# A graph network's edge gathers: counting by pairs of chunks, constants loaded ahead, five groups gathered ahead, and a shorter lag of the weights

## The chip, the cores and the metric

The kernel runs on one core of a Trainium2 chip. The core has five engines, each with its own instruction stream taken in order: TensorE (PE, matrix products, with a weight load that runs beside them, PEld), VectorE (DVE), ScalarE (ACT, functions of one operand), GpSimd (POOL, which also issues the indirect transfers that gather rows) and SyncE (SP, which issues most other transfers). They wait for each other through semaphores. Sixteen DMA engines move data between device memory (DRAM), the on-chip SBUF and, through the engines, PSUM. The metric is the device time of one execution in microseconds (us); lower is better.

## The reference, cut to what matters

A graph of 3,125 nodes and 100,000 edges, sorted by destination, with a low index far likelier as a destination than a high one. First a four-layer attention network with 8 heads of 16, then a second message network on the same edges.

```
h = gelu(x @ Wi.T + bi)
for i in range(4):
    q = (h @ Wq.T + bq)[dst]; k = (h @ Wk.T + bk)[src]; v = (h @ Wv.T + bv)[src]
    alpha = sum(q * k over 16) / 4                     # per edge and head
    ex = exp(alpha - segment_max(alpha, dst)[dst])
    out = segment_sum(ex / segment_sum(ex, dst)[dst] * v, dst)
    x_r = h @ Ws.T + bs
    beta = sigmoid([out, x_r, out - x_r] @ Wbeta.T)
    h = layer_norm(beta * x_r + (1 - beta) * out + h)
    h = gelu(h @ W1.T + b1) @ W2.T + b2 + h
x = layernorm(x + h @ Wo.T + bo)
msg = silu([x[src], x[dst], rbf(edge_weight)] @ mw1 + mb1) @ mw2 + mb2
agg = segment_sum(msg, dst) / max(count, 1)
x = layernorm(x + layer_norm(silu([x, agg] @ uw1 + ub1) @ uw2 + ub2))
```

## The kernel before

Nodes lie in 25 tiles of 128 (NT). Edges are cut into items of 256 (`IS`) that all have their destinations in one tile; an item is two chunks of 128 edges, one edge per partition. The lowest four tiles of destinations (DT), which take in many edges each, are treated densely: for them the kernel counts how often each source meets each destination and adds the logarithm of that count as a mask to a full attention of 512 destinations against all nodes. All other edges go through gathers: 246 items (SPI), 123 groups of four chunks (SPG) in each layer.

The stages follow each other in one program.

*Sorting* (`order_edges`, `sort_edges`) brings edges into items, and makes for each chunk of the dense tiles two numbers per edge (`place`, `last`, L452 on): which source row, and which column of a window of DW = 8 low destinations; the window's start for each chunk comes from a masked minimum (L436 to 439).

*Counting* (`count_edges`, L968): for each of 324 chunks POOL makes a one-hot of the source within its tile (`hot_l`, L987), DVE one of source tile times window column (`hot_w`, 25×8 = 200 wide, L990), PE multiplies them (`c_ps`, L993) and DVE adds the product into `cnt` at the window's place (L996), all written in one order with no step ahead of another but by three buffers. Between chunks, seven times, `enter` (L1416) takes four node tiles through the first linear layer, Gelu and the projections to k, v, q and x_r (`project`, `project_rest`). Then 28 blocks of masks are built: transposes of `cnt` on PE, L1008 and L1014 on DVE, L1012 and L1013 on ACT, and stored.

*Layers* (`layers`, L1436). Ahead of the first layer, and at the end of each node stage, the first AHEAD = 4 groups are gathered: four indirect transfers a group, each bringing 128 rows of k and v into a buffer `kvg` (L680). `attention` then runs `edge_sums` (L700), a pipeline by hand. Turn g of `range(-3, ng + LAG + 2)` issues:

```
at(g + 3, fetch)            # gather of group g+3, its row one-hots (hrows)
at(g - LAG - 2, add)        # sums into acc
others(per_turn * (g + 0.5))
at(g, scores)               # qk, alpha (DVE), ev copy of v out of kvg (ACT, L759)
at(g + 1, select)           # q_ps: q rows by one-hot (PE, L742)
advance()                   # one step of the maxima
others(per_turn * (g + 1))
advance()
at(g - LAG + 1, columns)    # hcols
at(g - LAG, weights)        # ev times ex (DVE, L779)
at(g - LAG - 1, by_node)    # products with hcols (PE, L794)
```

Softmax maxima are made for batches of GB = 8 groups by `Maxima.steps` (L559): a generator of some 13 steps, each on another engine than the one before, of which `advance` runs one. It transposes the scores, copies them on ACT (`at`, L577), scans over them on DVE (`fwd`, L581), goes forth and back once more, and ends in the exponentials `ex` (L628). A group's weights are due LAG = GB+6 = 14 turns after its scores. The dense attention (`dense_steps`, L852) is a list of 258 slots, `beside`, spread evenly over the turns by `others`: scores `d_ps` (PE, L878), mask and maximum (DVE, L888), exponentials (ACT, L901), transposes (`pt_ps`, PE, L910), copies (ACT, L917), products with v (L927). In layer 0 the row and column one-hots are made on DVE and stored; layers 1 to 3 load them on SP's queue.

*Node stage* (`node_stage`, L1290): the gate of attention and x_r (`mixing`, with its exponential `beta`, L1077), layer norm, two linear layers with Gelu (L1337, `u`), the next layer's projections. At its start SP loads `lng`, `lnb`, `w1`, `b1`, `w2`, `b2` and the next layer's weights. At its end the next layer's first four groups are gathered, and `project_rest` follows.

*Second network* (`second_network`, `messages`, L1456 on): 204 groups with 816 gathers (L680, `ag`).

The attention stands in two forms under a branch on what sorting found: the one described is taken when the items fit the tables and windows sized for them; the other, general, treats all edges by gathers.

## Time and profile before

| what | us |
|---|---|
| median of three runs (4751.56 to 4760.54) | 4754.53 |
| profiled execution | 4763.96 |
| its span, first to last instruction | 4762.1 |
| sorting, 0 to 83 | 83 |
| counting with entry, 83 to 346 | 263 |
| masks, 346 to 400 | 54 |
| layer 0, first to last gather | 717 |
| layers 1, 2, 3, first to last gather | 667, 661, 667 |
| between the gathers of two layers | 146, 135, 133 |
| from layer 3's last gather to the first of the second network | 146 |
| second network, first to last gather | 1049 |

The stages are read from what each engine does over time; the same lines of code come back four times, once for each layer, and totals mix them. In a window's row the busy time and instruction count of each engine stand in turn; PEclk is the TensorE clock that was granted as a share of full speed; DMA is the mean busy share of the sixteen engines. In a timeline row the brackets hold the engine's idle time just before, and what ended it. In a list of waits the numbers are total, times and longest. A row of a group of instructions has its shortest, median and longest duration in ns.

### The profile page before, as it was taken

How to read it: one execution, taken by the hardware profiler on the slowest of the kernel's cores; microseconds unless marked ns; L12 is line 12 of the kernel's file. 1: busy time of each engine (PE TensorE's matmuls, PEld its weight loads, DVE VectorE, ACT ScalarE, POOL GpSimd, SP SyncE). 2: the span in 40 equal slices, each digit the busy share in tenths (PEclk: the TensorE clock that was granted, in tenths of full speed). 3: DMA queues.
4: the chain of work that ended last, by engine and by line, in shares of the span. 5: the costliest groups of instructions: out<-in, count | busy, mean ns of one | idle time of the engine just before them, and what ended most of it. 6: DMA issues, size and time to landing. Idle time of an engine off the chain costs nothing. (4 is left out here: it accounts for less than half of the span.)

```text
span 4762.1 us, 85370 instructions
## 1 busy us (share of the span) xinstructions
PE 3845.5 (81%) x25947; PEld 2699.6 (57%) x25947; DVE 3246.7 (68%) x10137; ACT 1996.0 (42%) x3967; POOL 2981.0 (63%) x3136
## 2 busy tenths in 40 slices
PE   3666898987889998879999987999887766667775
PEld 1223665665456666546666654666664665666664
DVE  6775898987557987647787855788785444445644
ACT  0014454553345555435555542565543333233321
POOL 4664776762267777147777605777741777777775
PEclk9555998998879999979999996999898888888987
DMA  2005787885467887457887826888762333334432
GB/s 60 27 32 189 230 247 237 249 243 138 144 189 247 258 250 233 114 174 221 246 256 238 221 82 192 245 259 257 229 179 58 97 90 91 92 92 86 97 89 52
DMA packets 451834, 801.33 MB, mean 168 GB/s; under 512 B 93445, under 2 KB 175878, under 8 KB 451296
## 3 DMA queue, kind: packets, MB, share of 16 engines
q1 hardware_dynamic: 329488, 481.40, 31.7%
q0 software_dynamic: 121056, 313.06, 25.7%
q8 instruction: 229, 3.75, 0.3%
q14 instruction: 277, 2.27, 0.2%
q10 hardware_dynamic: 784, 0.85, 0.1%
HBM read 693.93 MB, written 102.26 MB: 167 GB/s over the span
## 5 line engine op out<-in xcount | busy, mean ns | idle before, releaser
L680 POOL DMA_INDIRECT kvg<-kv_d,src_i x1968 | 1955.9, 994 | 880.3 <-issue 567.8
L680 POOL DMA_INDIRECT ag<-a_d,src_i x816 | 797.0, 977 | 254.0 <-issue 226.4
L917 ACT COPY pt<-pt_ps 128x512 f32<-128x512 f32 (+1 forms) x832 | 470.7, 566 | 684.5 <-PE pt_ps L910 677.3
L910 PE MATMUL pt_ps<-ident,sm 128*128 128x128 f32 x3200 | 572.1, 301 | 138.6 <-ACT pt L917 94.1
L742 PE MATMUL q_ps<-q,hrows 128*128 x3936 | 617.2, 303 | 47.6 <-DMA hrows<-hrows_d 21.1
L888 DVE CUSTOM_DVE_ANT_0 sm<-d_ps,mask 128x512 f32<-128x512 f32 (+1 forms) x896 | 541.5, 623 | 143.8 <-PE d_ps L878 119.0
L910 PEld LDWEIGHTS pt_ps<-ident,sm 128*128 128x128 f32 x3200 | 362.6, 148 | 477.8 <-issue 198.7
L742 PEld LDWEIGHTS q_ps<-q,hrows 128*128 128x128 f32 x3936 | 547.0, 213 | 146.2 <-issue 112.7
L878 PE MATMUL d_ps<-kt,qz 32*128 32x512 f32 (+1 forms) x1792 | 602.3, 650 | 7.4 <-DVE mx L888 7.3
L794 PE MATMUL s_ps<-ev,hcols 128*128 128x136 f32 x3744 | 565.9, 294 | 17.5 <-issue 5.5
L901 ACT ACTIVATE sm<-sm,dtop 128x512 f32<-128x512 f32 (+1 forms) x896 | 547.2, 669 | 26.0 <-DVE dtop L895 25.2
L759 ACT COPY ev<-kvg 128x512 f32<-128x512 f32 x492 | 303.5, 618 | 551.9 <-DMA kvg<-kv_d,src_i 351.8
L794 PEld LDWEIGHTS s_ps<-ev,hcols 128*128 128x128 f32 x3744 | 499.5, 200 | 60.8 <-issue 37.8
L1510 PE MATMUL s_ps<-m,hcols 128*128 128x129 f32 x1632 | 277.2, 322 | 256.3 <-DVE acc L1519 234.6
L1502 DVE TENSOR_TENSOR m<-ag,m_ps 128x512 f32<-128x512 f32 x204 | 139.9, 687 | 407.8 <-DMA ag<-a_d,src_i 369.4
L1510 PEld LDWEIGHTS s_ps<-m,hcols 128*128 128x128 f32 x1632 | 248.0, 230 | 292.2 <-ACT m L1503 156.1
L754 DVE TENSOR_TENSOR qk<-q_ps,kvg 128x512 f32<-128x512 f32 x492 | 335.5, 682 | 94.1 <-PE q_ps L742 71.3
L927 PE MATMUL av<-pt,v 128*17 128x128 f32 x6400 | 373.8, 287 | 1.7 <-ACT pt L917 1.7
L810 DVE TENSOR_TENSOR acc<-acc,s_ps 128x136 f32 x936 | 266.4, 285 | 106.2 <-PE s_ps L794 96.8
L779 DVE TENSOR_TENSOR ev<-ev,ex 128x512 f32<-128x512 f32 x492 | 332.5, 683 | 8.9 <-ACT ex L628 8.8
L755 DVE TENSOR_REDUCE alpha<-qk 128x32 f32<-128x512 f32 x492 | 330.8, 672 | 2.3
L1503 ACT ACTIVATE m<-m 128x512 f32<-128x512 f32 x204 | 125.1, 628 | 430.6 <-DVE m L1502 422.6
(316 smaller groups left out, 5247.6 us busy)
## 6 DMA issues: line engine op xcount, KB each, us to landing
mask<-mask_d SPq DMA_DIRECT2D x384, 256.0 KB
hrows<-hrows_d SPq DMA_DIRECT2D x369, 256.0 KB
hcols<-hcols_d SPq DMA_DIRECT2D x369, 256.0 KB
hrow<-drow_d SPq DMA_DIRECT2D x327, 128.0 KB
kvg<-kv_d,src_i POOLq DMA_INDIRECT x1968
hrows_d<-hrows SPq DMA_DIRECT2D x123, 256.0 KB
hcols_d<-hcols SPq DMA_DIRECT2D x123, 256.0 KB
ag<-a_d,src_i POOLq DMA_INDIRECT x816
```

The costliest lines, as they stand in the source:

```text
L680: nc.gpsimd.indirect_dma_start(out=out[:, x, :], out_offset=None, in_=table[:], in_offset=bass.IndirectOffsetOnAxis(ap=s["src_i"][:, i:i + ...
L742: nc.tensor.matmul(qs[g][:, x, :], hot[:, c * P:(c + 1) * P], a["q"][:, bass.ds(tn["PE"][item_of(g, c)], 1), :], start=True, stop=True)
L754: nc.vector.tensor_mul(qk, qs.pop(g), kvg[:, :, :HID])
L779: nc.vector.tensor_mul(e[:, :, :, :DH], e[:, :, :, :DH], ex.unsqueeze(3).to_broadcast([P, IC, GH, DH]))
L794: nc.tensor.matmul(sums[g][:, c // IC], hot[:, c, :], ev[:, ORDER.index(c)].rearrange("p h d -> p (h d)"), start=(c % IC == 0), stop=(c % ...
L878: nc.tensor.matmul(s_ps[i][:, :n * P], qz[r, h % 2, d * P:(d + 1) * P], kt[r, c * P:(c + n) * P], start=True, stop=True)
L888: nc.vector.tensor_tensor_reduce(out=sm[:, i, :n * P], in0=s_ps[i][:, :n * P], in1=mask[:, :n * P], scale=1.0, scalar=-3.0e38, op0=ALU.add ...
L901: nc.scalar.activation(sm[:, i, :n * P], sm[:, i, :n * P], AF.Exp, scale=1.0 / DH ** 0.5, bias=live[u]["top"][:, i:i + 1])
L910: nc.tensor.transpose(t_ps[:, x, y, :], sm[:, y, t % NS * P:(t % NS + 1) * P], k.ident)
L917: nc.scalar.copy(pt[:, :n], live[u]["t_ps"].pop(i)[:, :n])
L927: nc.tensor.matmul(av[r:r + DX, u % len(PAIRS), :], v[:, t, h, :], pt[:, x, y, :], start=(i == 0), stop=(t + 2 >= NT))
L1510: nc.tensor.matmul(s_ps[:, c // IC, :], h[:, c, :], x[:, c, :], start=(c % IC == 0), stop=(c % IC == IC - 1))
```

## The change

1. Counting goes by items of two chunks, 162 of them. DW grows to 10, and there is one window for an item. Its start is no more a masked minimum: four indirect gathers on POOL fetch each chunk's first edge record, and DVE takes the destination out of it. `hot_l` is made on ACT for both chunks: two squares of the distance from iota, with the number as bias (its sign is turned in `place`), and one Relu of 1 − distance over both. `hot_w` is still made per chunk on DVE, 250 wide. Two products accumulate in PSUM and one addition follows. Sources are made two items ahead, places one ahead, additions one behind. `enter` becomes three steps a block, 21 in all, spread evenly.
2. `lng`, `lnb`, `b2`, `b1` for all layers and `w1` of layer 0 are loaded at the start of the program, on POOL's queue; node stages reload `w1` alone, on SP, ahead of the next layer's first gathers. The two DVE operations that prepare `w_out` and `w_xr` of the next layer move from the node stage's beginning to the end of its loop's `late` blocks (`gate`).
3. The first groups of layer 0 are gathered when counting ends, before the masks are built.
4. AHEAD is 5, and the gathers of group g+4 are issued at the head of turn g.
5. 14 dense slots are issued in the first turn, and the remaining 244 spread as before.
6. LAG is 12; a third `advance` runs in each turn; the ev copy moves out of `scores` into `values`, later in the turn.

```
-DW = 8
+DW = 10
...
-LAG = GB + 6
+LAG = GB + 4
...
+        c0 = C0 // P
+        m = NC - c0
+        at_first = one.tile([P, m], I32, name="at_first")
+        nc.vector.scalar_tensor_tensor(at_first, part_f[:, c0:], -3.0 * P, at_edge[:, c0:],
+                                       op0=ALU.mult, op1=ALU.add)
+        first_e = one.tile([P, m, 3], I32, name="first_e")
+        for c in range(m):
+            nc.gpsimd.indirect_dma_start(
+                out=first_e[:, c], out_offset=None,
+                in_=ed_d.rearrange("r s -> (r s)").unsqueeze(1),
+                in_offset=bass.IndirectOffsetOnAxis(ap=at_first[:, c:c + 1], axis=0))
...
-        nc.vector.tensor_scalar(local, ins, -1000.0, 1000.0, op0=ALU.mult, op1=ALU.add)
-        nc.vector.tensor_add(local, local, sl[:, 1, c0:])
         lo = one.tile([P, m], F32, name="lo")
-        nc.vector.tensor_reduce(lo, local, axis=AX.X, op=ALU.min)
+        nc.vector.tensor_copy(lo, first_e[:, :, 1])
+        nc.vector.tensor_sub(lo, lo, tile_f[:, c0:])
...
-        nc.vector.scalar_tensor_tensor(place[:, 0], place[:, 1], -float(P), sl[:, 0, c0:],
-                                       op0=ALU.mult, op1=ALU.add)
+        nc.vector.scalar_tensor_tensor(place[:, 0], place[:, 1], float(P), sl[:, 0, c0:],
+                                       op0=ALU.mult, op1=ALU.subtract)
...
+    def rows_of(g):
         if g >= AHEAD:
             gather_rows(nc, s, a, g)
+    def fetch(g):
...
-        evs[g] = work.tile([P, GC, HEADS, DX], F32, name="ev", bufs=LAG + 3)
-        nc.scalar.copy(evs[g][:, :, :, :DH],
-                       kvg[:, :, HID:].rearrange("p c (h d) -> p c h d", d=DH))
         if b == GB - 1 or g == ng - 1:
             exs[n] = work.tile([P, IC, IB * HEADS], F32, name="ex")
             todo.append((n, maxima.steps(n, exs.pop((n, "alpha")), exs[n])))
+    def values(g):
+        evs[g] = work.tile([P, GC, HEADS, DX], F32, name="ev", bufs=LAG + 3)
+        nc.scalar.copy(evs[g][:, :, :, :DH],
+                       a["kvg"][g % AHEAD][:, :, HID:].rearrange("p c (h d) -> p c h d", d=DH))
...
+    at_once = min(14, len(beside))
+    per_turn = (len(beside) - at_once) / (ng + 4)
...
     for g in turns:
+        at(g + AHEAD - 1, rows_of)
         at(g + 3, fetch)
         at(g - LAG - 2, add)
         at(g + 2, one_hot)
-        others(per_turn * (g + 0.5))
+        others(at_once + per_turn * max(0, g + 0.5))
         if early and early[0][0] <= g:
             early.pop(0)[1]()
         at(g, scores)
         at(g + 1, select)
         advance()
-        others(per_turn * (g + 1))
+        others(at_once + per_turn * max(0, g + 1))
+        at(g, values)
         advance()
         at(g - LAG + 1, columns)
         at(g - LAG, weights)
+        advance()
         at(g - LAG - 1, by_node)
...
-def count_edges(tc, k, s, mask_d, first, minus, beside):
+def count_edges(tc, k, s, mask_d, first, minus, beside, then):
...
-        for c in range(CF, CF + CC):
-            j = c - C0
-            at_c = c - CF
-            if at_c % TB == 0:
-                n = min(TB, CF + CC - c)
-                _, at = nc.values_load_multi_w_load_instructions(
+        ls, ws, cs, at = {}, {}, {}, {}
+        def sources(i):
+            j = CF - C0 + i * IC
+            far = work.tile([P, IC, P], F32, name="far")
+            for c in range(IC):
+                nc.scalar.activation(far[:, c], iota[:, :P], AF.Square,
+                                     bias=s["last"][:, 0, j + c:j + c + 1])
+            ls[i] = work.tile([P, IC, P], BF16, name="hot_l")
+            nc.scalar.activation(ls[i], far, AF.Relu, scale=-1.0, bias=k.ones[:, 0:1])
+        def places(i):
+            j = CF - C0 + i * IC
+            ws[i] = work.tile([P, IC, NT * DW], BF16, name="hot_w")
+            for c in range(IC):
+                nc.vector.tensor_scalar(ws[i][:, c], iota, s["last"][:, 1, j + c:j + c + 1], None,
+                                        op0=ALU.is_equal)
+        def product(i):
+            cs[i] = ps.tile([P, NT, DW], F32, name="c_ps")
+            l, w = ls.pop(i), ws.pop(i)
+            for c in range(IC):
+                nc.tensor.matmul(cs[i].rearrange("p t w -> p (t w)"), l[:, c], w[:, c],
+                                 start=(c == 0), stop=(c == IC - 1))
+        def add(i):
+            if i % TB == 0:
+                n = min(TB, CI - i)
+                j = (CF - C0) // IC + i
+                _, at["v"] = nc.values_load_multi_w_load_instructions(
                     s["window"][0:1, j:j + n], engines=[ET.DVE], min_val=0, max_val=DT * P - DW,
                     skip_runtime_bounds_check_because="windows are clamped when computed")
-            hot_l = work.tile([P, P], BF16, name="hot_l")
-            nc.gpsimd.tensor_scalar(hot_l, iota[:, :P], s["last"][:, 0, j:j + 1], None,
-                                    op0=ALU.is_equal)
-            hot_w = work.tile([P, NT * DW], BF16, name="hot_w")
-            nc.vector.tensor_scalar(hot_w, iota, s["last"][:, 1, j:j + 1], None,
-                                    op0=ALU.is_equal)
-            c_ps = ps.tile([P, NT, DW], F32, name="c_ps")
-            nc.tensor.matmul(c_ps.rearrange("p t w -> p (t w)"), hot_l, hot_w, start=True,
-                             stop=True)
-            o = cnt[:, :, bass.ds(at[at_c % TB], DW)]
-            nc.vector.tensor_add(o, o, c_ps)
-            upto = len(beside) * (at_c + 1) // CC
+            o = cnt[:, :, bass.ds(at["v"][i % TB], DW)]
+            nc.vector.tensor_add(o, o, cs.pop(i))
+        for i in range(-2, CI + 1):
+            for ahead, step in ((2, sources), (1, places), (0, product), (-1, add)):
+                if 0 <= i + ahead < CI:
+                    step(i + ahead)
+            upto = max(0, len(beside) * (i + 1) // CI)
             for step in beside[done:upto]:
                 step()
             done = upto
+        then()
...
-AHEAD = 4
+AHEAD = 5
...
-    nc.vector.tensor_add(a["w_out"][l % 2], wbeta[:, :HID], wbeta[:, 2 * HID:])
-    nc.vector.tensor_sub(a["w_xr"], wbeta[:, HID:2 * HID], wbeta[:, 2 * HID:])
+    def gate():
+        nc.vector.tensor_add(a["w_out"][l % 2], wbeta[:, :HID], wbeta[:, 2 * HID:])
+        nc.vector.tensor_sub(a["w_xr"], wbeta[:, HID:2 * HID], wbeta[:, 2 * HID:])
+    return gate
...
-        lng = wp.tile([P, 1], F32, name="lng")
-        nc.sync.dma_start(lng, w["ln_g"][l:l + 1, :].rearrange("o d -> d o"))
-        lnb = wp.tile([P, 1], F32, name="lnb")
-        nc.sync.dma_start(lnb, w["ln_b"][l:l + 1, :].rearrange("o d -> d o"))
-        w1 = wp.tile([P, 4 * HID], F32, name="w1")
-        nc.sync.dma_start(w1, w["w1t"][l])
-        b1 = wp.tile([P, 4], F32, name="b1")
-        nc.sync.dma_start(b1, w["b1t"][:, l * 4:(l + 1) * 4])
+        w1 = a["w1"]
+        lng, lnb, b2 = (t[:, l:l + 1] for t in (a["lng"], a["lnb"], a["b2"]))
+        b1 = a["b1"][:, 4 * l:4 * l + 4]
         w2 = wp.tile([P, 4, HID], F32, name="w2")
         nc.sync.dma_start(w2, w["w2t"][l].rearrange("(f p) o -> p f o", p=P))
-        b2 = wp.tile([P, 1], F32, name="b2")
-        nc.sync.dma_start(b2, w["b2"][l:l + 1, :].rearrange("o d -> d o"))
+        gate = None
         if l < 3:
-            layer_weights(tc, w, l + 1, a, wp)
+            gate = layer_weights(tc, w, l + 1, a, wp)
...
+            if i == len(late) and gate:
+                gate()
...
         if l < 3:
+            nc.sync.dma_start(w1, w["w1t"][l + 1])
             for g in range(AHEAD):
                 gather_rows(nc, s, a, g)
...
+        for name, table in (("lng", "ln_g"), ("lnb", "ln_b"), ("b2", "b2")):
+            a[name] = hp.tile([P, 4], F32, name=name)
+            nc.gpsimd.dma_start(a[name], w[table].rearrange("l d -> d l"))
+        a["b1"] = hp.tile([P, 16], F32, name="b1")
+        nc.gpsimd.dma_start(a["b1"], w["b1t"])
+        a["w1"] = hp.tile([P, 4 * HID], F32, name="w1")
+        nc.gpsimd.dma_start(a["w1"], w["w1t"][0])
+        a["kvg"] = [hp.tile([P, GC, 2 * HID], F32, name=f"kvg{i}") for i in range(AHEAD)]
...
+                x = {}
+                def begin():
+                    xt = work.tile([64, GC * P], F32, name="xt")
+                    nc.scalar.dma_start(xt[:, :n], w["x_t"][:, t:t + n])
+                    h_ps = ps.tile([P, GC * P], F32, name="h_ps")
+                    nc.tensor.matmul(h_ps[:, :n], wi, xt[:, :n], start=True, stop=True)
+                    x["ht"] = work.tile([P, GC * P], F32, name="ht")
+                    nc.scalar.activation(x["ht"][:, :n], h_ps[:, :n], AF.Gelu, bias=bi)
+                return [begin, lambda: project(tc, k, a, x["ht"], work, ps, tiles),
+                        lambda: project_rest(tc, k, a, x["ht"], work, ps, tiles)]
             with tc.tile_pool(name="in0p", bufs=1, space=PSUM) as ps:
                 count_edges(tc, k, s, s["mask_d"], first, minus,
-                            [lambda tiles=tiles: enter(tiles) for tiles in BLOCKS])
+                            [step for tiles in BLOCKS for step in enter(tiles)],
+                            lambda: [gather_rows(nc, s, a, g) for g in range(AHEAD)])
...
-    for g in range(AHEAD):
-        gather_rows(nc, s, a, g)
```

More of the change, by code (lines that the diff above doesn't have):

```diff
@@ L249, in sort_edges @@
     last = keep2.tile([P, 2, NCP - C0], F32, name="last")
-    window = keep2.tile([1, NCP - C0], I32, name="window")
+    window = keep2.tile([1, (NCP - C0) // IC], I32, name="window")
     begins_d = dram.tile([NIT, IS + 1], BF16, name="begins_d")
@@ L287, in sort_edges @@
         nc.vector.tensor_copy(at_i, at_f)
-        edge = one.tile([T1, IS, 3], I32, name="edge")
+        rec = one.tile([P, NC, P, 3], I32, name="rec")
+        edge = rec[:T1, :IC].rearrange("p c s j -> p (c s) j")
         nc.gpsimd.indirect_dma_start(
@@ L377, in sort_edges @@
                                 op1=ALU.mult)
-        rec = one.tile([P, NC, P, 3], I32, name="rec")
         for c in range(NC):
@@ L418, in sort_edges @@
         nc.sync.dma_start(drow_d.rearrange("(c p) s -> p c s", p=P), low)
-        w_s = one.tile([P, NC, P], F32, name="w_s")
+        w_s = tdiag
         nc.vector.tensor_copy(w_s, rec.bitcast(F32)[:, :, :, 2])
@@ L429, in sort_edges @@
             nc.vector.tensor_copy(dloc[:, c * P:(c + 1) * P], t_ps[:, 1, :])
-        c0 = C0 // P
-        m = NC - c0
         ins = inside[:, c0:]
         local = one.tile([P, m, P], F32, name="local")
-        nc.vector.tensor_scalar(local, ins, -1000.0, 1000.0, op0=ALU.mult, op1=ALU.add)
-        nc.vector.tensor_add(local, local, sl[:, 1, c0:])
         lo = one.tile([P, m], F32, name="lo")
-        nc.vector.tensor_reduce(lo, local, axis=AX.X, op=ALU.min)
+        nc.vector.tensor_copy(lo, first_e[:, :, 1])
+        nc.vector.tensor_sub(lo, lo, tile_f[:, c0:])
         nc.vector.tensor_scalar(lo, lo, float(P - DW), 0.0, op0=ALU.min, op1=ALU.max)
@@ L472, in sort_edges @@
                          tdiag[:, :m, :].rearrange("p c s -> p (c s)"), start=True, stop=True)
-        nc.vector.tensor_scalar_min(window, w_ps[:, :m * P], float(DT * P - DW))
+        nc.vector.tensor_scalar_min(window, w_ps[:, :m * P:IC], float(DT * P - DW))
         nb = (NIT + P - 1) // P
@@ L612, in steps @@
             nc.vector.tensor_scalar(gain, gain, self.s["goes_on"][:, n:n + 1], None, op0=ALU.mult)
-            node = work.tile([1, P], F32, name="node")
+            node = work.tile([1, P], F32, name="node", bufs=1)
             c = n * BC
@@ L714, in edge_sums @@
     rows, hots, qs, evs, cols, sums = {}, {}, {}, {}, {}, {}
-    def fetch(g):
+    def rows_of(g):
         if g >= AHEAD:
             gather_rows(nc, s, a, g)
+    def fetch(g):
         if kept == "load":
@@ L822, in edge_sums @@
     turns = range(-3, ng + LAG + 2)
-    per_turn = len(beside) / (ng + 4)
+    at_once = min(14, len(beside))
+    per_turn = (len(beside) - at_once) / (ng + 4)
     def at(g, step):
@@ L1411, in networks @@
             nc.scalar.dma_start(bi, w["bi"].rearrange("o d -> d o"))
-            layer_weights(tc, w, 0, a, one)
+            layer_weights(tc, w, 0, a, one)()
             s = sort_edges(tc, k, ed_d, consts, dram, one)
@@ L1417, in enter @@
                 t, n = tiles[0] * P, len(tiles) * P
-                xt = work.tile([64, GC * P], F32, name="xt")
-                nc.scalar.dma_start(xt[:, :n], w["x_t"][:, t:t + n])
-                h_ps = ps.tile([P, GC * P], F32, name="h_ps")
-                nc.tensor.matmul(h_ps[:, :n], wi, xt[:, :n], start=True, stop=True)
-                ht = work.tile([P, GC * P], F32, name="ht")
-                nc.scalar.activation(ht[:, :n], h_ps[:, :n], AF.Gelu, bias=bi)
-                project(tc, k, a, ht, work, ps, tiles)
-                project_rest(tc, k, a, ht, work, ps, tiles)
+                x = {}
[8 more added lines that the diff above has]
+                        lambda: project_rest(tc, k, a, x["ht"], work, ps, tiles)]
             with tc.tile_pool(name="in0p", bufs=1, space=PSUM) as ps:
                 count_edges(tc, k, s, s["mask_d"], first, minus,
-                            [lambda tiles=tiles: enter(tiles) for tiles in BLOCKS])
+                            [step for tiles in BLOCKS for step in enter(tiles)],
+                            lambda: [gather_rows(nc, s, a, g) for g in range(AHEAD)])
         with tc.tile_pool(name="net0acc", bufs=1) as ap:
             a["acc"] = ap.tile([P, NT, HEADS, DX], F32, name="acc")
-            a["kvg"] = [ap.tile([P, GC, 2 * HID], F32, name=f"kvg{i}") for i in range(AHEAD)]
             layers(tc, k, s, w, a, hp, dram, out)
```

## The prediction

> **What bounds the kernel now.** I read the page's totals first, then windows cut at the stage borders, then what the engines waited for where a window shows idle time.
>
> ```profile
> span 4762.1 us, 85370 instructions
> PE 3845.5 (81%) x25947; PEld 2699.6 (57%) x25947; DVE 3246.7 (68%) x10137; ACT 1996.0 (42%) x3967; POOL 2981.0 (63%) x3136
> ...
> L680 POOL DMA_INDIRECT kvg<-kv_d,src_i x1968 | 1955.9, 994 | 880.3 <-issue 567.8
> ```
>
> No engine is full over the span. But each gather is 0.99 us busy and most are followed by about 0.3 us of issue (567.8 us over 1,968): a pitch of 1.25 to 1.28 us, 630 us for one layer's 492 gathers. In layer 1 the first gather starts at 1263.4 and the last ends at 1930.0, so 667 us: gathers bound that stretch but for some 34 us. Now the stages:
>
> ```profile
> core 0: us, PE busy (x) PEld busy (x) DVE busy (x) ACT busy (x) POOL busy (x), PEclk, DMA share, GB/s
> 83.00:346.00 263.00, 174.69 (x478) 71.23 (x476) 201.56 (x771) 19.72 (x46) 188.86 (x324) 0.55 0.08 27
> 346.00:400.00 54.00, 29.08 (x102) 18.81 (x102) 34.63 (x61) 37.19 (x58) 0.01 (x1) 0.50 0.33 123
> ...
> 500.00:1130.00 630.00, 565.82 (x4475) 389.73 (x4477) 549.57 (x1572) 325.84 (x690) 445.40 (x424) 0.92 0.81 240
> ...
> 1263.00:1380.00 117.00, 85.02 (x372) 51.49 (x369) 59.37 (x207) 29.79 (x59) 68.93 (x72) 0.64 0.62 192
> 1380.00:1930.00 550.00, 516.84 (x4343) 359.52 (x4342) 452.42 (x1352) 312.75 (x673) 414.16 (x420) 0.97 0.80 244
> 1930.00:1984.00 54.00, 40.44 (x331) 32.76 (x332) 37.97 (x136) 18.00 (x49) 0.03 (x1) 0.91 0.45 99
> ```
>
> They are: counting with the entry of the nodes, the masks, the middle of layer 0, the start, middle and drain of layer 1. ACT does almost nothing while pairs are counted, POOL nothing while masks are built. In the middle of layer 1 POOL's 420 gathers take nearly all of 550 us, and PE is 94% busy too: little is to be had there. The start (POOL 69 of 117) and the drain have slack.
>
> ```profile
> L993 PE MATMUL c_ps<-hot_w,hot_l x324: 246/326/375, 84.4 to 345.4; 128*128 128x200 bf16 x162
> ...
>   POOL hot_l L987: 123.0, 240
>   DVE cnt L996: 48.4, 156
> ```
>
> In counting, PE sat idle 123.0 us for POOL's one-hot tile L987 and 48.4 us for DVE's addition: 324 chunks pass at the pace of POOL (0.60 us each, 188.9 in all), and stop during the seven entry blocks.
>
> ```profile
> ACT ev L759 <- DMA kvg<-kv_d,src_i: 61.2, 13, 14.2
> POOL kvg L680 <- issue: 30.4, 48, 10.0
> ...
> DVE fwd L581 <- ACT at L577: 18.2, 1, 18.2
> PEld pt_ps L910 <- ACT sm L901: 15.2, 2, 14.7
> ```
>
> ```profile
> 1344.88 0.94 POOL L680 DMA_INDIRECT kvg<-kv_d,src_i  x1 [6.74 <-ACT sm L901]
> ...
> 1364.69 0.94 POOL L680 DMA_INDIRECT kvg<-kv_d,src_i  x1 [9.97 <-issue]
> ```
>
> These are the waits of 1280 to 1380 and POOL's gaps there. ACT takes its instructions in order: twelve ev copies, each waiting for a gather (the last at 1335), stand ahead of the first maxima's `at` copy, for which DVE stops 18.2 us; meanwhile buffers stay occupied and POOL stops 6.4, 6.7 and 10.0 us. Layers 2 and 3 have the like (5.8, 6.7, 8.3 and 8.3, 6.7, 11.0).
>
> **Part by part.** The sum is made against the profiled execution: span 4762.1, time 4763.96, so 1.9 us lie around the span; it is 9.4 us above the median of the runs shown, 4754.53.
>
> Sorting: three DVE operations go (0.42, 0.68, 0.67 us = −1.8); four small indirect gathers join POOL behind the seven of rec, at L680's pitch 5 us, and a copy and a subtraction DVE. POOL is busy 20.9 of the first 83 us, and the gathers' consumer comes after the transposes and table stores, so I hide them. The five constant loads stand on POOL ahead of its first memset at 14.5 us, by the same pitch 6 us. If neither cover holds they cost 11. I take −1; ends −2 and +11.
>
> Counting: per item (two chunks) ACT now makes the source one-hots. Shapes are missing from the trace; the nearest are Gelu L1423 and Relu L1012, 0.37 us for 128x128 and 0.69 for 128x512, hence an estimate of 0.48 for 128x256: end to end 2×0.37+0.48 = 1.22 us. The low end is three copies at their means, 2×0.30 (L1157, 128x128) and 0.37 (L917, 128x256) = 0.97. Times 162 it is 157 to 198, plus the 19.7 ACT already has and two table loads of 1.28: 179 to 220. DVE: where it sets the pace now (327 to 328 us) a chunk takes 0.47 us, 0.19 of it until the addition starts and 0.28 after; a quarter wider, 324×0.24 = 77 and 162×0.35 = 57, with 29 of entry work 163. PE: 324×0.326×1.25 = 132 if each matmul stands alone, 101 if the wider ones take no longer than now (101.0), plus 73.7 of entry (174.7−101.0): 175 to 206. With sources two items ahead and the entry cut into 21 steps these lie beside each other; the longest, about 200, plus some 12 us of entry steps that still stop the line, gives 212, so −51. Ends: ACT's 179 with 9 us of stops, 188 (−75), and its 220 with twice the 12, 244 (−19).
>
> The trace has TensorE at a granted 0.55 there, and 19.92 us busy of 20 at 0.50 in 1300 to 1320. The Trainium skill, "TensorE: Matmul & The Clock Gate", Part 1, says about 3.4 us of sustained activity lifts the clock from half to full; by it a fuller PE would halve its term to about 100 and ACT alone would decide. The 20 busy microseconds at half clock speak against counting on it; by the rule the stage would end near 195, by the row at 212.
>
> The Trainium skill, "ScalarE: Activation LUTs", "What ACT_TABLE_LOAD costs", gives an ACTIVATE with pointer bias 280 ns + 0.833 ns per element, with 93 ns overlap of neighbours: an estimate of 0.99 us per item, inside my two ends. The same section adds 1.38 us of drain to every table switch, which speaks against the change, as the node stage gets four more; the trace shows loads of 1.283 us and no drain beside them. By the page the node stages would take 4×4×1.38 = 22 us more than in my sum.
>
> First rows: twenty gathers (25 us) move into the 54 us of masks, where POOL is idle. They share DMA with the mask stores (share 0.33): +1, ends 0 and +4. Layer 0 starts 20 gathers ahead; before, its first gather came at 400.0. But in 500 to 1130 PE is 90% and DVE 87% busy beside POOL's 71%, so in layer 0 the others hold POOL up (54 us of stalls, 717 us for the layer), and not all 25 reach the end; nor was the start waiting for gathers, as the first q_ps at 406.2 had waited 10.0 us for the hrow transfer, which comes no sooner. I take −12, a quarter of the stalls; ends −30 and 0.
>
> Layer starts 1 to 3: a fifth buffer removes the stall of 6.4 us outright (one more group is issued before the first buffer must come free) and 14 dense slots at once fill PE, which is idle 32 of 117 us. But the changed instruction order still puts the `at` copy on ACT behind twelve ev copies, now also behind 14 exponentials and about 11 pt copies, and DVE's fwd stands just ahead of qk(8). So the stall of batch 0 is moved and not removed: what is late next is POOL's group 13. Of 6.4+6.7+10.0 I take −12 per layer, −36; ends −25 and 0 each.
>
> Drains: weights run two turns sooner and a third step of the maxima runs per turn, so the last batch's chain (1954 to 1969 in the trace) ends sooner. The drain is 54 us for 16 turns, 3.4 us a turn; two turns less is 6.8, of which the chain's round trips keep some: −5 each, −20; ends −9 and 0 each.
>
> Node stages: six small loads go from SP, and layer norm's ht, which in the trace stood behind the beta activation until 1992.75 although t_ps was ready at 1983.7, no longer waits for it. Up to 9 us; ACT pays four more table loads, 5.1 us, and SP one reload of w1, which has a whole layer to land but stands ahead of the next layer's hrows loads. PE is busy 71 of 81 us, so most of the 9 was not on the path: −3 each, −12 for four; ends −9 and +5 each.
>
> Steady turns: three advances instead of two, values after the second dense share, gathers at the head of the turn: the same instructions, 0; ends −20 and +60 in all (the first a quarter of the small stalls of POOL past the starts, the second from the fourth rival). The second network isn't touched.
>
> Sum: −1−51+1−12−36−20−12 = −131. Span 4762−131 = 4631, time 4633; less the 9.4 by which the profiled run exceeds the median, **4624 us**.
>
> **The rivals.** *Counting alone pays.* For it: PE 94% and POOL full in the middle, and the `at` copy still behind the gathers. Against it: the 6.4 us stall has no other cause than buffers. −51 alone: about 4704.
>
> *More is won.* The start stalls go whole (−25 each), drains −9, counting ends at 195, layer 0 −25: −2−68−25−75−36−12 = −218, so 4536. For it: every start stall ends in a buffer coming free. Against: the order on ACT.
>
> *Slower.* In the turns, the third advance puts a step's dependent instructions on DVE, PE and ACT within one turn of the step that feeds them, and in-order DVE then waits for PE with weights and additions queued behind, for which by_node on PE waits. The nearest price is DVE's wait for PE in 1280 to 1380: 18.8 us in 8, 2.35 each. One more such wait per batch, 64 batches, is 150 us: 4624+150 = 4774. From 131 (2.0 us a batch) it is not faster. Against it: DVE is busy 452 of 550 us, so a turn of about 5.1 us has 0.9 us of slack, and gathered groups cover more. A partial one, 60, is the steady turn's upper end.
>
> *It doesn't do what it says.* Windows ten wide must hold 256 edges' low destinations; counted on the inputs the widest is exactly ten and the tables of items fit, so the fast arm is still taken. I give this nothing of its own.
>
> **The numbers.** Main case 0.60 (its own range 4565 to 4680), counting alone 0.17, more 0.12, slower 0.09, no change 0.02 (counting bound by ACT at 1.5 us an item, 243+22, and nothing else won). Half of the slack below 4540 and above 4715 may be left out: range 4540 to 4715. A change of 0.2% is about what a measurement of this kernel can tell from none. Faster 0.89, same 0.02, slower 0.09.
>
> **What would show it.** Counting 200 to 225 us long with PE's wait for POOL replaced by ACT; gathers inside the masks; layer 0 from first q_ps to last gather within 690 to 715 us (711 before); the 6.4 us stall gone at layers 1 to 3, one near 10 us left about group 13; drains near 48 us; ht within 2 us of t_ps; middle turns as before. The prediction falls if counting takes over 245 us, or if a middle turn grows by over 0.1 us.

## The result, and the profile after

The changed kernel takes 4695.41 us (4693.70 to 4700.52, four runs) against 4754.31 before: 0.9876 of it, 95% interval 0.9859 to 0.9893, so 59 us faster. 131 had been forecast: the time lies in the stated range, but 72 us of the forecast gain are missing. The profiled execution has these totals on its page:

```profile
span 4698.7 us, 84645 instructions
PE 3820.5 (81%) x25947; PEld 2695.1 (57%) x25947; DVE 3205.5 (68%) x9975; ACT 2183.8 (46%) x4470; POOL 2808.9 (60%) x2821
```

The stages are counting with entry, masks, and the start, middle and drain of layer 1 (busy time and count of each engine, clock, DMA). The first two rows are cut wider than the stages: counting itself runs from 85.5 to 296.0 us, and the last logarithm of the masks ends at 350.9.

```profile
76.00:299.00 223.00, 149.58 (x501) 69.63 (x502) 154.19 (x624) 182.46 (x536) 8.57 (x9) 0.70 0.12 39
299.00:365.00 66.00, 34.64 (x117) 20.75 (x115) 39.32 (x74) 39.03 (x61) 14.14 (x12) 0.51 0.47 159
1190.00:1310.00 120.00, 91.46 (x405) 50.19 (x403) 56.41 (x207) 37.05 (x65) 61.07 (x65) 0.67 0.57 176
1310.00:1864.00 554.00, 517.09 (x4328) 364.72 (x4326) 461.41 (x1355) 309.40 (x667) 422.30 (x428) 0.96 0.80 246
1864.00:1913.00 49.00, 37.39 (x312) 29.91 (x313) 36.19 (x133) 17.03 (x47) 0.22 (x1) 0.90 0.41 96
```

ACT now carries counting (182.5 us busy where it had 19.7). The middle of layer 1 is much as it was: POOL near its pace, PE at 93%. But in the start of layer 1 POOL is busy 61 of 120 us, and was 69 of 117. The same borders read off all stages give this account, in us, with the terms of the prediction beside it and the best of the experiments below, the changed kernel with its dense slots spread evenly. A drain runs from a layer's last gather to the first transpose of its node stage (`t_ps`):

| stage | forecast | changed kernel | dense slots even |
|---|---|---|---|
| sorting, to the first hot_w | −1 | +2.2 | +1.2 |
| counting, to the last addition | −51 | −52.5 | −54.0 |
| masks | +1 | +1.4 | +1.8 |
| layer 0, masks to last gather | −12 | −23.7 | −30.0 |
| layers 1 to 3, first to last gather | −36 | **+38.9** | −33.1 |
| four drains, to the first t_ps | −20 | −9.5 | 0.0 |
| four node stages, to the next gather | −12 | −18.5 | −18.6 |
| second network and after | 0 | −2 | −4 |
| span | −131 | −63.4 | −137.0 |

Each entry is a difference of two times in the traces; for instance counting before runs from 83.3 to 346.2, after from 85.5 to 296.0. One large row has the wrong sign: layers 1 to 3 got longer, by 7.5, 19.4 and 12.0 us. More than all of it lies between a layer's first gather and that of group 24: 147.6, 141.5 and 146.4 us before, 162.0, 165.9 and 165.4 after, 58 us more in all; the rest of the three layers gives 19 of them back. These are the engines' waits early in layer 1 of the changed kernel (1205 to 1290: total, times, longest):

```profile
ACT ev L776 <- DMA kvg<-kv_d,src_i: 41.9, 9, 12.4
POOL kvg L690 <- issue: 33.7, 37, 10.4
DVE sm L907 <- PE d_ps L897: 18.9, 9, 3.9
PEld d_ps L897 <- DVE mx L907: 16.0, 9, 7.6
...
DVE sm L907 <- DMA mask<-mask_d: 9.1, 3, 4.6
```

In the kernel before, the same two engines waited like this (1280 to 1380):

```profile
DVE sm L888 <- PE d_ps L878: 18.8, 8, 4.9
...
PEld d_ps L878 <- DVE mx L888: 1.6, 5, 0.7
```

DVE's wait for PE's d_ps is no longer than it was. New is PE's wait for DVE's maximum, 16.0 us for 1.6: each of the two d_ps has one buffer, so the next block can't be written before DVE has read the last, and the dense blocks go back and forth one at a time. Three of DVE's blocks first wait for their mask to arrive, 9.1 us. TensorE's own row of events shows what stands behind it:

```profile
1214.36 2.68 PE L897 MATMUL d_ps<-kt,qz 32*128 32x512 f32 x4 [6.74 <-DVE mx L907]
1217.22 2.07 PE L897 MATMUL d_ps<-kt,qz 32*128 32x512 f32 x2 [0.18 <-DVE mx L907]
1219.22 3.78 PE L754 MATMUL q_ps<-q,hrows 128*128 x16
```

The first q_ps comes at 1219.2, 29 us after the first gather, behind these blocks in PE's order; before, it came 22.8 us after it. POOL waits for the buffers:

```profile
1222.76 0.94 POOL L690 DMA_INDIRECT kvg<-kv_d,src_i  x1 [7.68 <-issue]
1227.32 0.94 POOL L690 DMA_INDIRECT kvg<-kv_d,src_i  x1 [3.61 <-DMA kvg<-kv_d,src_i]
...
1262.96 0.94 POOL L690 DMA_INDIRECT kvg<-kv_d,src_i  x1 [10.39 <-issue]
...
1280.16 0.94 POOL L690 DMA_INDIRECT kvg<-kv_d,src_i  x1 [6.59 <-ACT pt L936]
```

The first of these waits ends when qk of group 0 has read its rows (1221.33 to 1222.02), behind that q_ps. The longest, 10.39 us, ends with qk of group 5. Its q_ps was done by 1243.8, but on DVE a dense block stood ahead of it and waited for a buffer of sm, until PE had transposed an earlier block; and PE waited for ACT, where 13 exponentials and a copy stand in one piece from 1250.8 to 1259.0:

```profile
1259.06 1.12 PE L929 MATMUL pt_ps<-ident,sm 128*128 128x128 f32 x4 [3.97 <-ACT pt L936]
```

```profile
1260.31 0.69 DVE L907 CUSTOM_DVE_ANT_0 sm<-d_ps,mask 128x512 f32<-128x512 f32 x1 [11.96 <-PE pt_ps L929]
...
1261.54 0.69 DVE L766 TENSOR_TENSOR qk<-q_ps,kvg 128x512 f32<-128x512 f32 x1
```

In the kernel before, qk of group 5 starts 46 us after the first gather; here 71.

### The profile page after: what moved, and what is told of

The parts are those of the page before. It is cut to its first block, busy times and chain, and to the rows that moved or that the text cites. A ratio compares the mean times of both kernels' runs of the same rounds, so it can differ in the third digit from the quotient of the medians.

```text
span 4698.7 us, 84645 instructions
## 1 busy us (share of the span) xinstructions
PE 3820.5 (81%) x25947; PEld 2695.1 (57%) x25947; DVE 3205.5 (68%) x9975; ACT 2183.8 (46%) x4470; POOL 2808.9 (60%) x2821
## 5 line engine op out<-in xcount | busy, mean ns | idle before, releaser
L808 PEld LDWEIGHTS s_ps<-ev,hcols 128*128 128x128 f32 x3744 | 500.2, 200 | 45.2 <-issue 23.7
```

Of the source, the lines that this page charges most:

```text
L808: nc.tensor.matmul(sums[g][:, c // IC], hot[:, c, :], ev[:, ORDER.index(c)].rearrange("p h d -> p (h d)"), start=(c % IC == 0), stop=(c % ...
```

## The experiments

Eighteen runs were made. Four fell on chips like the first, where the kernel before takes 4755 to 4759 us; fourteen on chips where it takes 5950 to 6030. There the gathers don't set the pace of a layer's middle (620 to 660 us for 445), so those runs are read for places in the trace more than for time.

**The turn's parts undone one by one.** Theory A: the 14 dense slots at once delay the first groups. Theory B: the new order within a turn does.

```
e1 and its repeats    - at_once = min(14, len(beside))
                      + at_once = 0                    # others(per_turn * (g + 0.5)) as before
e2                    LAG = GB + 6, one advance() less, AHEAD = 4
e3                    at(g, values) directly behind at(g, scores)
e4                    AHEAD = 4
```

> The changed kernel, but the 258 dense slots spread evenly over the turns as before (none at once). In layers 1 to 3 of the changed kernel the first qk comes 31 to 34 us after the first gather and the ninth at 96 to 100, against 24 to 25 and 56 to 58 before. Theory A (the 14 slots at once put scores d_ps on PE and sm on DVE ahead of the first qk, so buffers come free later): the ninth qk returns to about 60 us, layers 1 to 3 get 12 to 20 us shorter each, about 4650. Theory B (the late start comes from the order within the turn, that is values behind the second dense share and the third advance): within 8 us of the changed kernel's 4695, or slower by the PE work that is no longer done in the idle start.

> The changed kernel with a lag of 14 and two advances a turn (as before), and four groups gathered ahead, since 17 ev buffers and five kvg buffers don't fit together. Read it against the run with four groups ahead alone. Theory A: the drains lose the two turns again, 7 to 11 us at each of four layers, so 25 to 40 us slower than that run. Theory B: the start of layers 1 to 3 gets better by 10 us or more each and outweighs this: equal or faster than that run.

> The changed kernel, but the ev copy stands directly behind scores again, ahead of the second dense share. Theory A: the ninth qk stays at 90 to 100 us, the time within 8 us of 4695. Theory B: the start of layers 1 to 3 is 10 us shorter each, about 4665.

> The changed kernel with four groups gathered ahead in place of five. If the fifth buffer is worth what the prediction gave it (the first stall of 6.4 us at a layer's start), it is 15 to 25 us slower than 4695; if the starts are bound by when qk and ev release buffers, the first gathers just wait one group sooner and the time is within 8 us.

All four fell on a slower chip, with 6029 us before: in this order 0.9882 (0.9846 to 0.9917), 0.9828 (0.9784 to 0.9872), 0.9887 (0.9858 to 0.9916) and 0.9871 (0.9826 to 0.9916) of it. The expected times can't be held against these, but e2 can be held against e4, on the same chip: 30 us faster, where theory A expected 25 to 40 slower. The two intervals overlap, and e11 and e12 below, the same pair with even slots, differ by 24 us the other way; so these times decide nothing. In the traces only the even spread changes the starts: group 13 of layers 1 to 3 is gathered 92 to 96 us after the first, in the three others 115 to 120. That is theory A's place, and the two orders tried for theory B, the third advance and the ev copy, show nothing there; the gathers at the head of the turn were not tried alone. With four buffers (e4) group 13 comes 116 to 118 us after the first gather, with five and 14 slots at once (e3) 115 to 116.

**Control, even spread, counting alone, constants.**

```
e5   the changed kernel, unaltered
e6   the kernel before, with counting by items alone (layers, AHEAD, LAG, constants as before)
e8   lng, lnb, b1, b2, w1 loaded in every node stage again, w_out and w_xr prepared there
```

> The changed kernel itself, unaltered, as the control for the other runs on this chip. The first four runs fell on a chip where the kernel before took 6029 us, so their times can't be set against the changed kernel's 4695. On a chip like the first it takes about 4695 (0.9876 of the kernel before); on one like the second, 0.985 to 0.992 of the kernel before.

> The changed kernel with the dense slots spread evenly, again, beside the control. In the run on the slower chip the gathers of group 13 began 92 to 96 us after a layer's first, against 115 to 120 in the three runs with 14 slots at once. Theory A: layers 1 to 3 are 8 to 20 us shorter each than the control's, so 25 to 60 us faster than it. Rival: what the start wins the steady turns give back, as each has 2.03 dense slots instead of 1.92; then the middle of a layer (group 24 to 110) is longer by about as much and the time within 10 us of the control.

> The kernel before with only the counting by items (windows ten wide, one-hots of sources on ACT, entry in 21 steps, the first records gathered). Theory A, with most of the gain made ahead of layer 0 by counting: 40 to 55 us faster than before, that is 4700 to 4715 where before takes 4754. If a good part of the changed kernel's 72 us up to the end of layer 0 comes from gathering ahead, less than 40.

> The changed kernel with the constants loaded in each node stage as before (and w_out and w_xr prepared at its beginning). Between the last gather of a layer and the first of the next the changed kernel has 145.5, 124.2 and 124.7 us against 146.4, 135.2 and 133.4 before. If the constants make these gains: 8 to 12 us longer at each of two or three of these gaps, 20 to 30 us slower than the control. If the shorter lag alone makes them: within 8 us of the control.

Again a slower chip (6013 us): e5 0.9891 (0.9841 to 0.9941), e1b 0.9920 (0.9893 to 0.9946), e6 0.9917 (0.9890 to 0.9945), e8 0.9957 (0.9935 to 0.9979). The rival's pattern holds there: even slots shorten the starts to group 24 by 10 to 15 us a layer and lengthen the middles by 23 to 38, and the sum is no faster than the control.

**Gathers after the masks** (e7; the edit in short).

```
-  then()                              # count_edges, ahead of the masks
+  gather_rows for each g < AHEAD      # layers, behind the masks
```

> The changed kernel with the first rows of layer 0 gathered after the masks, as before. In the changed kernel group 24 of layer 0 is gathered at 496 us (on the first chip), 45 us sooner than before, of which 35 are the earlier end of the masks. If gathering beside the masks makes the other 10: about 10 us slower than the changed kernel, layer 0's middle as in it. If it also makes the 20 us by which the middle of layer 0 got shorter: 25 to 30 us slower. If PE and DVE hold POOL up there anyway: within 6 us.

A chip like the first: 4688.69 against 4755.05, 0.9862 (0.9844 to 0.9880); the interval overlaps the changed kernel's. The trace says why nothing is lost: the first gather still starts at 286.6 us, in the changed kernel at 287.8. POOL has nothing else to do in the masks, so the place in the program doesn't matter to it. What held the gathers back in the kernel before is where their buffers lie:

```profile
399.99 1.03 POOL L680 DMA_INDIRECT kvg<-kv_d,src_i  x1 [54.79 <-ACT log L1013]
```

There the buffers are allotted only behind counting and masks, and the first gather waits for the masks' last logarithm; the changed kernel allots them at the start of the program, which the list of changes doesn't name. In the run with counting alone (e6b), which keeps the old place, the first gather waits for the masks again, until 348.2. So e7 didn't undo the effect, and what the early gathers are worth was not measured by itself. Its expectation also took the masks to end 35 us sooner; their last logarithm ends at 350.9 instead of 399.7, 49 us sooner.

**The same three on a chip like the first.**

> The changed kernel with the dense slots spread evenly, on a chip where the kernel before takes about 4755 (if it falls on one). On the slower chip the starts of layers 1 to 3 (first gather to group 24) were 12 to 15 us shorter than the control's and the middles (group 24 to 110) 23 to 38 us longer, the middles there being far from POOL's pace. Theory A: where gathers set the pace of the middle the start's gain of 12 to 20 us a layer stays, 4640 to 4660. Rival (PE's work is only moved): the middles grow by as much, within 10 us of 4695.

> The kernel before with only the counting by items, on a chip where it takes about 4755 (if it falls on one). On the slower chip the first gather of layer 0 came at 348.7 us, where it came at 400.0 before on the first chip. Theory A: 45 to 55 us faster than before, 4700 to 4710, so nearly the whole gain of the changed kernel; the layers as before. Rival: part of it is lost in layer 0, where PE and DVE are the bound: 20 to 40 us.

> The changed kernel with the constants loaded in each node stage, on a chip where the kernel before takes about 4755 (if it falls on one). On the slower chip it took 50 us more than the control by the medians, but its gaps between the layers only 3 to 4 us more each. If the constants make the gains of the gaps: 10 to 20 us slower than 4695. If the shorter lag makes them: within 6 us.

Against 4759.20 before, on one chip:

| kernel | us | of before | interval |
|---|---|---|---|
| changed, slots even | 4629.98 | 0.9740 | 0.9724 to 0.9757 |
| before, counting alone | 4708.91 | 0.9907 | 0.9887 to 0.9928 |
| changed, constants in each stage | 4720.93 | 0.9927 | 0.9910 to 0.9943 |

The even spread is the fastest kernel of the study, 129 us under the kernel before and, between two chips, 65 under the changed one. That bears theory A out, with a time below its window of 4640 to 4660, and the rival falls here: its middles (group 24 to 110) are 446, 445, 445 us, the changed kernel's 445, 446, 446. Its waits early in layer 1 (1198 to 1283) lack the train: PE waits for DVE's maximum 0.6 us where it waited 16.0.

```profile
ACT ev L776 <- DMA kvg<-kv_d,src_i: 47.0, 10, 8.1
DVE fwd L591 <- ACT at L587: 18.7, 1, 18.7
PEld m_ps L564 <- DVE fwd L591: 18.5, 1, 18.5
...
POOL kvg L690 <- issue: 16.1, 47, 2.1
...
DVE sm L907 <- PE d_ps L897: 10.2, 9, 2.3
...
PEld d_ps L897 <- DVE mx L907: 0.6, 2, 0.4
```

PE takes scores and q rows in turn without a pause between them:

```profile
1206.86 2.05 PE L754 MATMUL q_ps<-q,hrows 128*128 x8 [7.22 <-DMA hrows<-hrows_d]
1208.84 2.08 PE L897 MATMUL d_ps<-kt,qz 32*128 32x512 f32 x4
1210.85 2.08 PE L754 MATMUL q_ps<-q,hrows 128*128 x8
```

Here the first q_ps comes 23.6 us after the first gather, released by the hrows transfer, and the ninth qk 59 us after it, in the changed kernel 96. POOL's long waits at the start fall from 7.7, 3.6, 10.4 and 6.6 us to 2.1, 3.6 and 8.2:

```profile
1210.37 0.94 POOL L690 DMA_INDIRECT kvg<-kv_d,src_i  x1 [2.12 <-issue]
1214.93 0.94 POOL L690 DMA_INDIRECT kvg<-kv_d,src_i  x1 [3.61 <-DMA kvg<-kv_d,src_i]
...
1266.53 0.94 POOL L690 DMA_INDIRECT kvg<-kv_d,src_i  x1 [8.15 <-ACT pt L936]
```

Counting alone gives 50 us of the medians, and its layers are the kernel before's (starts to group 24: 148, 144, 142 us). The constants, with the place of the two operations for `w_out` and `w_xr`, are worth 25 us between two chips' medians; 15 of them stand in the node stages, 3.1, 4.3, 5.5 and 2.2 us each from the first t_ps to the next gather, and a further 5 in the second network, which nothing here touches, so 15 to 20 is the safer figure. The two parts were not told apart by time. In the kernel with constants in each stage ACT waits as before:

```profile
1924.00 0.20 ACT L1120 ACTIVATE beta<-beta 128x4 f32<-128x4 f32 x1 [14.05 <-DMA lnb<-in_ln_b]
1926.07 0.20 ACT L1120 ACTIVATE beta<-beta 128x4 f32<-128x4 f32 x1 [1.87 <-DVE beta L1115]
1926.18 1.43 ACT L1373 ACTIVATE ht<-t_ps,lnb,lng 128x512 f32<-128x512 f32 x2
```

In the changed kernel ht follows its transposes (t_ps at 1912.8) at once; then comes a table load (ACT_TABLE_LOAD in the rows), and nothing between it and the work it was for:

```profile
1913.51 1.45 ACT L1371 ACTIVATE ht<-t_ps,lnb,lng 128x512 f32<-128x512 f32 x2 [7.89 <-PE t_ps L1369]
1914.97 1.28 ACT L1378 ACT_TABLE_LOAD   x1
1916.27 0.69 ACT L1378 ACTIVATE u<-u_ps,b 128x512 f32<-128x512 f32 x1
```

**By what way the slots delay the starts, and the fifth buffer.**

```
e9         at_once = min(4, len(beside))
e10, e10b  at_once = 0, others(per_turn * max(0, g - 8 + 0.5)), per_turn = len(beside) / (ng - 4)
e11, e11b  slots even, AHEAD = 4
e12        slots even, AHEAD = 4, LAG = GB + 6, two advances a turn
```

> The changed kernel with 4 dense slots at once instead of 14. In its trace each score block d_ps of the early slots waits for DVE's maximum of the one before (16.0 us in 9 waits, layer 1), because d_ps has one buffer a head, and q_ps stands behind it in PE's order. If the cost is this train of waits, it is about in proportion to the slots: 14 cost 65 us, 4 cost 10 to 25, so 4640 to 4655. If the price is paid by the first slots alone (the first mask's transfer, which comes late), nearly all of it stays: 4675 to 4695.

> The changed kernel with no slot at once and the whole train of dense slots held back for 8 turns, then spread evenly over the rest. If the dense slots are what delays the first groups, the starts of layers 1 to 3 (first gather to group 24) get shorter than the 134 to 138 us of the even spread, by 5 to 15, and the time 4600 to 4630. If the start is bound by the gathers and the first maxima instead, the starts stay and the middle, with 2.17 slots a turn, is longer: 4630 to 4660.

> Even spread (4630) with four groups gathered ahead. If the fifth buffer is worth its 6 us at each start of layers 1 to 3, as the prediction had it: 4645 to 4655. If nothing: within 5 us of 4630.

> Even spread with four groups ahead and a lag of 14 with two advances a turn. Against the run with four groups ahead alone: if the shorter lag shortens four drains by 5 us each, as predicted, 20 us slower; if the third advance costs the middle of the layers as much, equal; if it costs more, faster.

> The dense slots held back for 8 turns and spread over the rest, on a chip where the kernel before takes about 4755 (if it falls on one). On the slower chip the starts of layers 1 to 3 came to 166 to 171 us from first gather to group 24, against 179 to 182 with the even spread and 192 to 195 with 14 at once, and the middles were no longer. If it carries over: 5 to 10 us a layer less than the even spread's 4630, so 4600 to 4620. If the middle, at 2.17 slots a turn, becomes PE's: 4630 to 4660.

> Even spread with four groups ahead, on a chip where the kernel before takes about 4755 (if it falls on one). On the slower chip the fifth buffer showed no gain (starts to group 24 of 180 to 181 us with four, 179 to 182 with five). If it is worth the 6 us at each start that the prediction gave it: 4645 to 4655. If nothing: within 5 us of 4630.

All six fell on slower chips: e9 0.9934 (0.9906 to 0.9961), e10 0.9891 (0.9860 to 0.9921), e11 0.9859 (0.9827 to 0.9891), e12 0.9892 (0.9853 to 0.9932) with 6030 us before, and e10b 0.9877 (0.9827 to 0.9926), e11b 0.9866 (0.9810 to 0.9923) with 5949. Times tell little there. The mean time from first gather to group 24 in layers 1 to 3, over kernels on these chips, does: 168 and 165 us with the slots held back, 180 with the even spread, 187 with 4 at once, 193 with 14. The more dense slots stand ahead of the first groups, the later these come, and the first four cost more each (1.7 us) than the ten after (0.7); so neither a price in proportion to the slots nor the first mask's transfer alone fits. With even slots four buffers and five have the same starts (179 to 181 us and 180 to 182 by each run's mean). Whether that and the gain of holding back carry over to a chip where gathers set the pace stays open.

The same traces price the drains. The shorter lag, with its third advance, takes 15 us (e4 against e2) and 22 us (e11 against e12) from the four drains together. The fifth buffer adds to them: four drains take 216 and 219 us with four buffers and even slots (e11, e11b), 229 and 238 with five (e1b, e1). In the program's order AHEAD = 5 puts a layer's last gather one turn sooner than 4 does, so one turn more of the same work lies behind it.

## Why the prediction was wrong, point by point

**The step that failed** is in the part on the layer starts: "14 dense slots at once fill PE, which is idle 32 of 117 us". Idle time of PE was read as room. But PE's gap at a layer's start is part of a chain (q_ps and the gathered rows, qk, buffer free, next gather), and what is put in the gap stands ahead of that chain in PE's and DVE's order, with round trips of its own: PE's d_ps for DVE's maximum, and a little later DVE's next block for PE's transposes and ACT's exponentials. The prediction saw these exponentials, but only ahead of the first maxima's `at` copy on ACT; the blocks ahead of q_ps on PE and ahead of qk on DVE it gave no price. The term was −36, with 0 as its worst end; it measured +39, and −33 with this one part taken out. That −33 lies near −36, but not all of it is the forecast's: 27 of it stand in the starts to group 24, 10 in the middles, for which 0 was forecast, and the ends give 4 back. The five buffers and the order of the turn were not measured one by one on a chip like the first. "Removes the stall of 6.4 us outright" was wrong as well: the stall came one group later and was 7.7 us; with even slots it is 2.1. The even spread loses 9.5 us in the drains, perhaps because fewer slots are left there when 14 are done early; that is far less than the 72 us it wins in layers 1 to 3.

**Counting** was right in time, −51 forecast and −52.5 in the trace, and partly by luck. The longest engine was to be at about 200 us, with PE at 175 to 206, and 12 us of stops beside it. In the 210 us of the trace PE is busy 143 us and ACT, the longest, 181, the low end of its range; the stops are 29. PE's waits name the new pace:

```profile
L1022 PE MATMUL c_ps<-hot_w,hot_l x324: 267/388/415, 88.3 to 295.1; 128*128 128x250 bf16 x162
...
  ACT hot_l L1009: 54.5, 87
  issue: 46.9, 74
  DVE cnt L1033: 20.7, 18
  ACT far L1006: 13.4, 14
```

POOL's 123.0 us became ACT's 54.5 + 13.4; 46.9 us are idle time for which the profile shows no cause (15.0 before). An item takes ACT 0.98 us, the low end of the 0.97 to 1.22 worked out:

```profile
88.07 0.68 ACT L1006 ACTIVATE far<-iota_b,last 128x128 f32<-128x128 bf16 x2
88.65 0.49 ACT L1009 ACTIVATE hot_l<-far,ones 128x256 bf16<-128x256 f32 x1
89.05 0.68 ACT L1006 ACTIVATE far<-iota_b,last 128x128 f32<-128x128 bf16 x2
```

The estimate from the Trainium skill's figures ("ScalarE: Activation LUTs", "What ACT_TABLE_LOAD costs"), 0.99 us, fits this to a hundredth. The same section's drain of 1.38 us with every switch of tables doesn't show here: in the rows above, the load starts 0.01 us after ht ends, and u 0.02 us after the load. On the clock, TensorE was granted 0.70 in counting on average, between the 0.55 of before and full speed. The stage took 210 us, near the 212 of the row and not the 195 of the rule in "TensorE: Matmul & The Clock Gate", Part 1; but PE's 143 us lie between the two, and ACT was the longest, as the rule would have had it, so this doesn't decide for the row.

**Sorting** cost 2.2 us where −1 was forecast, inside its ends: POOL's first gather of rec starts 1.3 us later (41.09 for 39.79); where the rest comes from isn't shown. **Masks** were right (+1.4). **Layer 0** was mis-sized, and its mechanism isn't shown: −24 (−30 with slots even) for −12, though inside its ends of −30 and 0. Counted from the masks' last logarithm, group 24 is gathered 4 us later than before, and with slots even 22 us sooner: the 14 slots at once cost the lead here too, but layer 0 wins nearly all of it back further on. What the gathers ahead, five buffers and the turn's order each gave was not told apart. From first q_ps to last gather the layer took 684 us, under the 690 to 715 named as a sign. **The drains** were mis-sized: −9.5, and 0 with slots even, for −20. Layers 1 to 3 gave 5.1, 3.5 and 3.6 us, near the 5 forecast for each, layer 0 none (67 us before, 70 after). The prediction counted two turns fewer, and not that the fifth buffer puts the last gather one turn sooner; on the slower chips the shorter lag and the fifth buffer pull the drains apart by amounts of the same size. **The node stages** gave 18.5 for 12, 15 of it by the mechanism named, as the run with constants in each stage shows: ht no longer stands behind beta, and the four more table loads of each stage don't lengthen it. **The steady turns** came out near the 0 forecast: the middles of layers 1 to 3 got 3 to 4 us shorter each, so the slower rival's round trips of the third advance didn't come. **The rival "counting alone pays"**, at 4704, is nearest in time to 4695, but by a different sum: layer 0, the drains and the node stages paid too, and layers 1 to 3 took 39 back.

## What to carry to other kernels

Before filling an idle engine, ask what it is idle for: work put into a gap stands in that engine's order ahead of the work the gap was waiting for, and costs its own round trips on top. At the start of a pipeline the first items set when buffers come free, so filler belongs among them or behind them, not ahead. Where several edits are made at once, one that loses can hide in a sum that wins: here it took half of it, 65 of 129 us.

## What the runs showed of the hardware

The kernel before took 4755 us on some chips and 5950 to 6030 on others, the changed one 4695 and 5939. In the changed kernel sorting and counting were alike (85.5 and 210.4 us on the first chip, 84.1 and 209.3 on the slower one), and a gather's mean was 1.000 us on both; the layers were not. These rows are 100 us of the middle of layer 1 in the changed kernel, on the first chip and on a slower one:

```profile
1400.00:1500.00 100.00, 96.54 (x853) 68.58 (x852) 86.42 (x248) 61.95 (x127) 76.22 (x79) 1.00 0.83 259
```

```profile
1600.00:1700.00 100.00, 80.31 (x552) 54.50 (x551) 57.27 (x155) 36.94 (x73) 56.76 (x59) 0.81 0.57 177
```

TensorE's granted clock was 0.81 instead of 1.00, a third fewer matmuls were done, and no engine was full (PE 80%, the others under 58%). On such a chip a change to POOL's pace can't be judged, and the cause was not found.
